# A planned instruction order, planned again with other durations: four graph layers on one core

## The chip, the cores and the metric

The kernel runs on one core of one Trainium2 chip. The core has a matrix engine (TensorE, PE in the profile; its weight loads are listed apart as PEld), a vector engine (VectorE, DVE), a scalar engine (ScalarE, ACT), GpSimd (POOL) and a queue for transfers (SyncE, SP). They run side by side and wait for each other through semaphores. The metric is the time of one execution on the device, in microseconds (us).

## The reference, cut to what matters

128 graphs of 64 nodes with 256 features go through four layers in float32. Each layer ends with a residual and a layer norm.

```python
# layer 0: a gated unit, five rounds with the same gates and another message weight each
A = (adj != 0)
h = x
for l in range(5):
    m = einsum('bnd,de->bne', h, weight[l])
    agg = einsum('bij,bid->bjd', A, m)
    h = gru_cell(agg, h, w_ih, w_hh, b_ih, b_hh)
x = layernorm(x + h * mask)
# layer 1: neighbour sum, then a two-layer network with RMS norm and SiLU, 256 -> 1024 -> 256
agg = epsilon * x + adj @ x
x = layernorm(x + silu(rmsnorm(agg @ W1 + b1)) @ W2 + b2)
# layer 2: log map, neighbour sum, exponential map, projection onto a ball (norms, artanh, tanh)
x = layernorm(x + project(expmap0(adj @ logmap0(x))))
# layer 3: attention with weights mask * exp(e_i + f_j), rows normalized
h = x @ W_w.T + W_b
x = layernorm(x + (u / u.sum(-1)) @ h)        # u = adj * exp(logits)
```

## The kernel before

The graphs form 16 groups of 8. A group is one stream of operations: five gated rounds, the network, the log and exponential maps, the attention, and four layer norms. Groups don't depend on each other except through shared buffers and the eight banks of matmul output. Nothing is issued while the program is described: each operation is put down with its engine, an estimated duration, and what it reads and writes. Some operations (copies out of the banks, scaled copies, the rows of a norm) can be done by ScalarE or VectorE and are put down with both.

```python
def dve(n, run, w, r):
    flow.op("DVE", 0.16 + 0.00105 * n, run, w, r)
def act(n, run, w, r):
    flow.op("ACT", 0.27 + 0.00077 * n, run, w, r)
def copied(n, o, i, w, r):
    flow.either([("ACT", 0.27 + 0.00077 * n, lambda: nc.scalar.copy(o(), i())),
                 ("DVE", 0.16 + 0.00105 * n, lambda: nc.vector.tensor_copy(o(), i()))], w, r)
def scaled(n, o, i, scale, bias, w, r):
    flow.either([("ACT", 0.27 + 0.00077 * n, lambda: nc.scalar.activation(o(), i(), AF.Identity, bias=bias(), scale=scale())),
                 ("DVE", 0.16 + 0.00105 * n, lambda: nc.vector.tensor_scalar(o(), i(), scale(), bias(), OP.mult, OP.add))], w, r)
```

A planner then plays the program forward with these durations. `clock` is when each engine is next free, `at` when an operation's inputs are there. At every step it takes the operation that can start first; ties, and the choice between groups, go by a rank. From the end of one operation to the start of one that needs it on another engine, a passing (`hop`) is added.

```python
            for s in range(self.first, min(self.first + flow.WINDOW, len(self.queues))):
                for e, q in self.queues[s].items():
                    opened = False
                    for _, o in zip(range(flow.AHEAD[e]), q):
                        t = max(clock[e], at[o.id])
                        # ... a free bank, or a free transfer slot, where o needs one
                        key = (t + o.ways[e][0] - min(w[0] for w in o.ways.values()) if len(o.ways) > 1 else t, *rank(s, o))
                        if best is None or key < best[0]:
                            best = key, o, e, t
            # ...
            end = t + o.ways[eng][0]
            clock[eng] = end
            # ...
            for u in o.then:
                need[u.id] -= 1
                at[u.id] = max(at[u.id], end + flow.hop(eng, u.eng))

    HOPS = {"from PE": 0.25, "to PE": 0.3, "else": 0.1}
    WINDOW, STRETCH, WIDTH, LAG = 4, 25.0, 8, 40.0
    ENDGAME = 350.0

    def hop(self, e, to):
        if e == to:
            return 0.0
        return self.HOPS["from PE" if e == "PE" else "to PE" if to == "PE" else "else"]
```

Up to four groups are open at once (`WINDOW`). The search keeps 8 partial plans (24 in the last 350 us of matmul work), lets each go on for a stretch under three different ranks, and keeps those with the lowest bound on the end. The best plan fixes the order of issue on each engine and the engine of each shared operation. The chip then runs that order; real durations and real semaphores decide the times.

```python
        ranks = (lambda s, o: (s, o.n), lambda s, o: (s if o.kb else -s, o.n), lambda s, o: (self.LAG * s - o.way, s, o.n))
        plans, until = [Plan(self)], 0.0
        while any(p.left for p in plans):
            late = until > self.work - self.ENDGAME
            until += self.STRETCH / 2 if late else self.STRETCH
            found = {}
            for p in plans:
                for rank in ranks:
                    c = p.copy()
                    if c.advance(until, rank):
                        found.setdefault((round(c.bound(), 3), c.left), c)
            plans = [found[k] for k in sorted(found)[:self.WIDTH * (3 if late else 1)]]
```

A layer norm is, for four rows of blocks `b`: two small DVE operations per block for mean and variance, one more, a power on POOL, the offset on DVE, and four shared operations for the rows.

```python
            for b in range(NB):
                dve(256, lambda b=b: nc.vector.bn_stats(st[:, b, :], y[:, b, :]), [(st, b)], [(y, b)])
                dve(4, lambda b=b: nc.vector.bn_aggr(mv[:, b, :], st[:, b, :]), [(mv, b)], [(st, b)])
            # ... variance + eps on DVE
            pool(1.1, lambda: nc.gpsimd.tensor_tensor(rstd[:, :m, :], ve[:, :m, :], pow2[:, :m, :], OP.pow), [rstd], [ve])
            # ... offset on DVE
            for b in range(NB):
                scaled(256, lambda b=b: o[:, b, :], lambda b=b: y[:, b, :], lambda b=b: rstd[:, 0, b:b + 1],
                       lambda b=b: off[:, b:b + 1], [(o, b)], [(y, b), off, rstd])
```

Names that return below: `p_u`, `p_v`, `p_w`, `p_r`, `p_in`, `p_hn` are banks of the gated rounds; `hnb`, `hr` are shared copies out of such banks; `U`, `V`, `Z`, `R` hold the gates; `tA`, `tB` and `t` are sums and differences made by DVE as matmul inputs; `ps_hid`, `p_1h`, `p_uh`, `p_vh`, `p_wh`, `hid`, `ps_o`, `xb` belong to the network; `ser`, `fac`, `tan`, `ps_sup` to the maps; `ps_a`, `hw`, `ps_att` to the attention; `x_n` are the rows of a norm.

Of the kernel before, what the change touches and what calls it, by code (L numbers as in the profile page):

```python
# [13 lines left out]
AF = mybir.ActivationFunctionType  # L14
OP = mybir.AluOpType
# [37 lines left out]
class Plan:  # L53
# [25 lines left out]
    def advance(self, until, rank):  # L79


        flow, need, at, clock, banks = self.flow, self.need, self.at, self.clock, self.banks
        while self.left and clock["PE"] < until:
            best = None
# [5 lines that stand above are left out]
                        if o.opens is not None:  # L90
                            if opened or not banks or need[o.id]:
                                opened = True
                                continue
                            t = max(t, banks[0])
                        elif need[o.id]:
                            continue
                        elif o.kb and e != "POOL":
                            t = max(t, self.lands[0])
                        key = (t + o.ways[e][0] - min(w[0] for w in o.ways.values()) if len(o.ways) > 1 else t, *rank(s, o))
                        if best is None or key < best[0]:  # L100
                            best = key, o, e, t
            if best is None:
                return False
            _, o, eng, t = best
            for e in o.ways:
                self.queues[o.stream][e].remove(o)
            self.order.append((eng, o))
            end = t + o.ways[eng][0]
            clock[eng] = end
            if eng == "PE":  # L110
                self.done += o.us
            if o.opens is not None:
                banks.pop(0)
            for b in o.bufs:
                n = self.uses.get(b, b.left) - 1
                self.uses[b] = n
                if not n:
                    banks.append(end + flow.hop(eng, "PE"))
                    banks.sort()
            if o.kb:  # L120
                self.bus = max(self.bus, end + flow.DMA[0]) + o.kb / flow.DMA[1]
                end = self.bus + flow.DMA[2]
                if o.eng != "POOL":
                    self.lands = [*self.lands[1:], end]
# [3 lines that stand above are left out]
            self.left -= 1  # L128
            while self.first < len(self.queues) and not any(self.queues[self.first].values()):
                self.first += 1  # L130
        return True
# [12 lines left out]
class Flow:  # L144
# [10 lines left out]

    AHEAD = {"PE": 32, "DVE": 10, "ACT": 10, "POOL": 4, "SP": 2}

    HOPS = {"from PE": 0.25, "to PE": 0.3, "else": 0.1}


    DMA = (2.0, 330.0, 1.0)
# [51 lines left out]

    def hop(self, e, to):
        if e == to:
            return 0.0
        return self.HOPS["from PE" if e == "PE" else "to PE" if to == "PE" else "else"]

    def ways(self):
# [41 lines left out]
def kernel(  # L261
# [31 lines left out]
    nc = tc.nc  # L293
# [19 lines left out]
    flow = Flow(tc)  # L313
# [6 lines left out]
    def bank(name):  # L320
        return Buf(lambda: psum.tile([P, 512], F32, tag="bank", name=name), bank=True)
# [4 lines left out]
    def unit(tag, s, name, shape=(P, R), bufs=1):  # L326

        t = f"{tag}{s}"
        return Buf(lambda: work.tile(list(shape), F32, tag=t, name=name, bufs=bufs), slot=(t, bufs))


    def matmul(o, lhsT, rhs, k, nk):
        return nc.tensor.matmul(o, lhsT, rhs, start=(k == 0), stop=(k == nk - 1))  # L333

    def pe(n, run, w, r):
        flow.op("PE", {512: 0.86, 256: 0.435, 128: 0.23, 1: 0.21}.get(n, 0.3), run, w, r)
# [2 lines left out]
        flow.op("PE", 0.11, run, w, r)  # L339

    def dve(n, run, w, r):
        flow.op("DVE", 0.16 + 0.00105 * n, run, w, r)

    def act(n, run, w, r):
        flow.op("ACT", 0.27 + 0.00077 * n, run, w, r)

    def copied(n, o, i, w, r):

        flow.either([("ACT", 0.27 + 0.00077 * n, lambda: nc.scalar.copy(o(), i())),  # L349
                     ("DVE", 0.16 + 0.00105 * n, lambda: nc.vector.tensor_copy(o(), i()))], w, r)  # L350

    def scaled(n, o, i, scale, bias, w, r):

        flow.either([("ACT", 0.27 + 0.00077 * n, lambda: nc.scalar.activation(o(), i(), AF.Identity, bias=bias(), scale=scale())),  # L354
                     ("DVE", 0.16 + 0.00105 * n, lambda: nc.vector.tensor_scalar(o(), i(), scale(), bias(), OP.mult, OP.add))], w, r)

    def pool(us, run, w, r=()):
        flow.op("POOL", us, run, w, r)
# [161 lines left out]
    for l in range(L):  # L520
        ps = bank("ps_wmT")
# [9 lines left out]
        for k in range(KD):  # L531
            for i, n in ((0, 2 * D), (1, D)):
                ps = bank("ps_wmih")
# [78 lines left out]
    def group(g):  # L612
        s = g % NF

        def tiny(name, shape=(P, NB), dt=F32):
            t = f"{name}{s}"
            return Buf(lambda: small.tile(list(shape), dt, tag=t, name=f"{name}_{g}"), slot=(t, 2))

        def u(tag, name, shape=(P, R)):
            return unit(tag, s, f"{name}_{g}", shape, bufs(tag))  # L620

        def rows(tag, name):
            return u(tag, name, (P, NB, D))
# [14 lines left out]
        def rows_of(src, n):  # L638

            ps = bank("ps_hr")  # L640
            for j in range(2):
                for c in range(KD):
                    turn(lambda j=j, c=c: nc.tensor.transpose(  # L643
                        ps[:, j * D + c * P:j * D + (c + 1) * P],
                        src[:, c, (2 * n + j) * P:(2 * n + j + 1) * P], ident.tile()), [ps], [(src, n)])
            return ps
# [46 lines left out]
        if g == NG - 2:  # L693


            for k in range(KD):
                w = unit("h", (NG - 3) % NF, f"w1_{k}", (P, H), 2)
# [4 lines left out]
        ps = bank("ps_adjT")  # L702
# [129 lines left out]
        for n in range(2):  # L832
            ps = rows_of(hT, n)
            for j in range(2):
                b = 2 * n + j
# [91 lines left out]
        ps = bank("ps_ss")  # L927
# [10 lines left out]
        for c in range(KH):  # L938
# [4 lines left out]
            th = u("VZR"[c % 3], f"th{c}")  # L943
# [5 lines left out]
        for h in range(NB // 2):  # L949
            ps = bank("ps_o1")  # L950
            for j in range(2):
                b = 2 * h + j
# [4 lines left out]
            for j in range(2):  # L957
                b = 2 * h + j
                dve(256, lambda ps=ps, b=b, j=j: nc.vector.scalar_tensor_tensor(
                    y1[:, b, :], ps[:, j * D:(j + 1) * D], 0.5, xb[:, b, :], OP.mult, OP.add), [(y1, b)], [ps, (xb, b)])  # L960
        xn = tiny("n")
        x2 = layer_norm(y1, "A", "n1", xn)


        rn, fac, n2, ser = (tiny(t) for t in ("rn", "fac", "n2", "ser"))
        near = tiny("near", dt=I32)
# [11 lines left out]
        def series():  # L978
# [5 lines left out]
                  for q in (11, 9, 7, 5, 3)),  # L984
                v.tensor_add(ser.tile(), ser.tile(), one4),
                v.scalar_tensor_tensor(near.tile(), xn.tile(), SERIES_BELOW, one4, OP.is_lt, OP.mult)]
        dve(1250, series, [n2, ser, near], [xn])
        dve(4, lambda: nc.vector.scalar_tensor_tensor(fac.tile(), fac.tile(), 0.5, rn.tile(), OP.mult, OP.mult),
            [fac], [fac, rn])
        dve(4, lambda: nc.vector.copy_predicated(fac.tile(), near.tile(), ser.tile()), [fac], [fac, near, ser])  # L990
        tan = rows("B", "tan")
        for b in range(NB):
            flow.either([
                ("DVE", 0.37, lambda b=b: nc.vector.tensor_scalar(tan[:, b, :], x2[:, b, :], fac[:, b:b + 1], None, OP.mult)),
                ("ACT", 0.47, lambda b=b: nc.scalar.activation(tan[:, b, :], x2[:, b, :], AF.Identity, scale=fac[:, b:b + 1]))],
                [(tan, b)], [(x2, b), fac])
        us = tiny("ss")
        sup = [bank("ps_sup") for _ in range(NB // 2)]
        for h in range(NB // 2):
            for j in range(2):  # L1000
                b = 2 * h + j
                pe(256, lambda b=b, j=j, ps=sup[h]: matmul(
                    ps[:, j * D:(j + 1) * D], adjT[:, b, :], tan[:, b, :], 0, 1), [sup[h]], [adjT, (tan, b)])
            for j in range(2):
                b = 2 * h + j
# [3 lines left out]
        un, unb, th, urn = tiny("n"), tiny("n2"), tiny("th"), tiny("rn")  # L1009
# [12 lines left out]
                v.scalar_tensor_tensor(un.tile(), un.tile(), MAX_NORM, one4, OP.mult, OP.min),  # L1022
                v.tensor_mul(th.tile(), th.tile(), un.tile())]
        dve(4, lambda: nc.vector.reciprocal(urn.tile(), unb.tile()), [urn], [unb])
        dve(800, onto_ball, [th, un], [th, un, urn])
        y2 = rows("y", "y2")
        for b in range(NB):
            dve(256, lambda b=b, ps=sup[b // 2]: nc.vector.scalar_tensor_tensor(
# [11 lines left out]
        for b in range(NB):  # L1040
            ps = bank("ps_a")
            for k in range(KD):
                pe(256, lambda ps=ps, b=b, k=k: matmul(
                    ps[:, :D + 2], x3T[:, k, b * P:(b + 1) * P], wattT[:, k, :], k, KD), [ps], [(x3T, b // 2), wattT])
            act(4, lambda ps=ps, b=b: nc.scalar.activation(
                hw[:, b, D:], ps[:, D:D + 2], AF.Exp, bias=cs.tile()), [(hw, b)], [ps, cs])
            flow.either([
                ("ACT", 0.47, lambda ps=ps, b=b: nc.scalar.activation(
                    hw[:, b, :D], ps[:, :D], AF.Identity, scale=hw[:, b, D:D + 1])),
                ("DVE", 0.43, lambda ps=ps, b=b: nc.vector.tensor_scalar(  # L1050
                    hw[:, b, :D], ps[:, :D], hw[:, b, D:D + 1], None, OP.mult))], [(hw, b)], [ps, (hw, b)])
        dve(1030, lambda: nc.vector.tensor_add(x3.tile(), x3.tile(), over(wb_r.tile(), NB)), [x3], [x3, wb_r])
        y3 = rows("y", "y3")
# [1 line left out]
        for b in range(NB):  # L1055
            ps = bank("ps_att")
# [7 lines left out]
        o = layer_norm(y3, "A", "n3")  # L1064
# [38 lines left out]
```

## Time and profile before

| | |
|---|---|
| time, median of 3 | 2431.84 us (2430.58 to 2432.48) |
| span of the profiled execution | 2430.5 us |
| PE, PEld busy | 99%, 87% |
| DVE, ACT, POOL busy | 78%, 47%, 8% |
| mean granted TensorE clock | 0.994 |
| mean DMA rate | 15 GB/s |

A line of a group reads: line and engine, operation, what it writes and reads, shapes, count, then busy time and mean duration of one in ns, then the idle time of the engine ahead of it and what ended that. Records overlap on an engine, as the next operation may start before the last one has been recorded as ended, so the distance between starts says more than the duration. Two groups that can run on either engine show this division of work before:

```profile
L354 ACT ACTIVATE hnb<-p_hn,half_b 128x256 f32<-128x256 f32 x232 | 101.6, 472 | 81.4 <-PE p_hn L663 67.4 <-DVE hnb L355 13.0 <-DVE Z L776 0.7
...
L354 ACT ACTIVATE x_n<-y,off,rstd 128x256 f32<-128x256 f32 x78 | 42.9, 593 | 44.2 <-DVE off L684 44.1
```

```profile
L355 DVE TENSOR_SCALAR hnb<-p_hn,half_b 128x256 f32<-128x256 f32 x88 | 41.4, 480 | 19.6 <-PE p_hn L663 10.7 <-ACT hnb L354 8.5
L355 DVE TENSOR_SCALAR x_n<-y,rstd,off 128x256 f32<-128x256 f32 x114 | 40.8, 409 | 0.5
```

### The profile page before, as it was taken

The page shows a single profiled execution, that of the slowest core. Times are in us where ns is not written, and L with a number is a line of the kernel's source. Part 1 is how long each engine was busy: PE and PEld are TensorE (multiplying, and loading weights), DVE is VectorE, ACT ScalarE, POOL GpSimd, SP SyncE. Part 2 cuts the span into 40 slices and gives each one's busy share as a digit, 9 for nine tenths or more (in the row PEclk, how much of TensorE's full clock was granted, in tenths as well). Part 3 has the DMA queues.
Part 4 walks back from the last instruction along what each step waited for, and adds up shares of the span by engine and source line. Part 5 has one row for each costly group of instructions (what it writes and reads, how often), then busy time and mean ns, then how long its engine had stood idle before and what let it go on. Part 6 is the DMA issues. An engine that isn't in the chain of part 4 may idle for free.

```text
span 2430.5 us, 32703 instructions
## 1 busy us (share of the span) xinstructions
PE 2394.7 (99%) x12258; PEld 2102.9 (87%) x12258; DVE 1893.4 (78%) x4097; ACT 1147.1 (47%) x2408; POOL 188.2 (8%) x144
## 2 busy tenths in 40 slices
PE   9999999999999999999999999999999999999995
PEld 7888888888888888888888888888888888888864
DVE  3668787887888877778777887888787787878777
ACT  4434544444444444454444545455444544445453
POOL 4000000000100000000000100000000000000011
PEclk9999999999999999999999999999999999999997
DMA  4000000000000000000000000000000000000000
GB/s 127 3 1 12 1 29 1 18 12 1 29 1 27 3 18 11 1 27 3 16 14 1 29 1 27 3 19 11 1 29 1 18 12 1 27 9 18 9 9 18
DMA packets 39725, 36.21 MB, mean 15 GB/s; under 512 B 9956, under 2 KB 38656, under 8 KB 39568
## 3 DMA queue, kind: packets, MB, share of 16 engines
q1 hardware_dynamic: 37840, 32.25, 4.2%
q8 instruction: 97, 1.59, 0.3%
q10 hardware_dynamic: 1328, 1.31, 0.2%
q0 software_dynamic: 400, 0.57, 0.1%
q14 instruction: 60, 0.49, 0.1%
HBM read 25.74 MB, written 8.39 MB: 14 GB/s over the span
## 4 chain that ended last, share of the span: by engine, by line
PE 94%; DVE 4%; ACT 1%; DMA 1%; issue 0%; POOL 0%; SPq 0%; POOLq 0%; ACTq 0%; DVEq 0%
PE p_v L663 11%; PE p_w L663 11%; PE p_in L663 11%; PE p_r L663 11%; PE p_hn L663 11%; PE ps_o L333 9%; PE ps_agg L333 6%; PE p_u L663 6%; PE ps_hr L643 3%; PE ps_a L333 2%; PE p_wh L882 2%; PE p_vh L882 2%; PE p_1h L882 2%; PE ps_T L633 1%; PE ps_att L333 1%; PE p_uh L882 1%
## 5 line engine op out<-in xcount | busy, mean ns | idle before, releaser
L663 PE MATMUL p_hn<-hT,w_hn 128*128 128x256 f32 x1280 | 322.8, 380 | 0.0
L663 PE MATMUL p_in<-agg,w_in 128*128 128x256 f32 x1280 | 315.4, 379 | 0.0
L663 PEld LDWEIGHTS p_in<-agg,w_in 128*128 128x128 f32 x1280 | 240.2, 190 | 31.1
L663 PEld LDWEIGHTS p_hn<-hT,w_hn 128*128 128x128 f32 x1280 | 227.9, 191 | 22.7
L333 PE MATMUL ps_o<-w2s,hid 128*128 128x256 f32 x1024 | 231.2, 379 | 0.0
L333 PEld LDWEIGHTS ps_o<-w2s,hid 128*128 128x128 f32 x1024 | 193.9, 190 | 27.3 <-issue 1.2
L678 POOL TENSOR_TENSOR rstd<-ve,pow 128x4 f32<-128x4 f32 (+1 forms) x64 | 82.5, 1289 | 1491.6 <-DVE ve L676 1484.0
L767 ACT ACTIVATE V<-V,half_b 128x256 f32<-128x256 f32 x160 | 72.7, 500 | 199.2 <-DVE V L763 199.0
L663 PE MATMUL p_u<-tA,s 128*128 128x256 f32 x640 | 158.1, 381 | 1.4 <-DVE tA L746 0.6
L663 PE MATMUL p_w<-tA,s 128*128 128x256 f32 x640 | 158.1, 379 | 0.0
L663 PE MATMUL p_r<-hT,a 128*128 128x256 f32 x640 | 156.9, 379 | 0.0
L663 PE MATMUL p_r<-agg,a 128*128 128x256 f32 x640 | 156.7, 379 | 0.0
L663 PE MATMUL p_v<-tB,s 128*128 128x256 f32 x640 | 155.4, 379 | 0.0
L663 PE MATMUL p_v<-tB,na 128*128 128x256 f32 x640 | 154.5, 379 | 0.0
L663 PE MATMUL p_w<-hT,s 128*128 128x256 f32 x640 | 154.3, 379 | 0.0
L349 ACT COPY agg<-ps_agg 128x512 f32<-128x512 f32 x154 | 89.9, 584 | 114.2 <-PE ps_agg L333 98.8
L333 PEld LDWEIGHTS ps_agg<-edge,hr 128*128 128x128 f32 x1024 | 136.1, 191 | 6.6
L354 ACT ACTIVATE hnb<-p_hn,half_b 128x256 f32<-128x256 f32 x232 | 101.6, 472 | 81.4 <-PE p_hn L663 67.4
L333 PE MATMUL ps_agg<-edge,hr 128*128 128x128 f32 x1024 | 138.8, 275 | 0.0
L663 PEld LDWEIGHTS p_u<-tA,s 128*128 128x128 f32 x640 | 119.3, 190 | 21.0 <-DVE tA L746 2.3
L663 PEld LDWEIGHTS p_v<-tB,s 128*128 128x128 f32 x640 | 120.9, 190 | 16.3 <-PE ps_att L333 0.2
L663 PEld LDWEIGHTS p_w<-hT,s 128*128 128x128 f32 x640 | 120.7, 190 | 16.0
(233 smaller groups left out, 4686.5 us busy)
## 6 DMA issues: line engine op xcount, KB each, us to landing
x<-in_x_dram SPq DMA_DIRECT2D x16, 512.0 KB, 3.6
xr<-in_x_dram SPq DMA_DIRECT2D x16, 512.0 KB, 3.6
out_dram<-x_n SPq DMA_DIRECT2D x16, 512.0 KB, 2.9
edge<-in_adj_dram SPq DMA_DIRECT2D x32, 64.0 KB, 2.3
wm<-in_L_gnn_weight_dram SPq DMA_DIRECT2D x5, 256.0 KB, 5.3
w2s<-in_L_gnn_W_dram SPq DMA_DIRECT2D x1, 1024.0 KB, 10.0
w<-in_L_gnn_W_dram SPq DMA_DIRECT2D x2, 512.0 KB, 3.5
w_in_L_gnn_w_hh_dram<-in_L_gnn_w_hh_dram ACTq DMA_DIRECT2D x1, 512.0 KB, 5.2
```

What stands on the lines that cost most here:

```text
L333: return nc.tensor.matmul(o, lhsT, rhs, start=(k == 0), stop=(k == nk - 1))
L349: flow.either([("ACT", 0.27 + 0.00077 * n, lambda: nc.scalar.copy(o(), i())), ("DVE", 0.16 + 0.00105 * n, lambda: nc.vector.tensor_copy(o( ...
L354: flow.either([("ACT", 0.27 + 0.00077 * n, lambda: nc.scalar.activation(o(), i(), AF.Identity, bias=bias(), scale=scale())), ("DVE", 0.16 ...
L633: turn(lambda j=j, c=c: nc.tensor.transpose(ps[:, c * HR + j * P:c * HR + (j + 1) * P], src[:, 2 * n + j, c * P:(c + 1) * P], ident.tile() ...
L643: turn(lambda j=j, c=c: nc.tensor.transpose(ps[:, j * D + c * P:j * D + (c + 1) * P], src[:, c, (2 * n + j) * P:(2 * n + j + 1) * P], iden ...
L663: pe(256, lambda c=c, k=k: nc.tensor.matmul(ps[:, c * HR:(c + 1) * HR], w[:, k, c * P:(c + 1) * P], v(k), start=first and c == k == 0, sto ...
L678: pool(1.1, lambda: nc.gpsimd.tensor_tensor(rstd[:, :m, :], ve[:, :m, :], pow2[:, :m, :], OP.pow), [rstd], [ve])
L767: act(256, lambda c=c: nc.scalar.activation(o[:, c, :], src(c), AF.Tanh, bias=half_b[:, i * KD + c:i * KD + c + 1], scale=0.5), [(o, c)], ...
L882: pe(256, lambda c=c: nc.tensor.matmul(ps[:, c * HR:(c + 1) * HR], w1f[:, w, (2 * q + c) * P:(2 * q + c + 1) * P], v[0](), start=first and ...
```

## The change

The planner gets other constants. Operations of DVE and ACT get shorter fixed parts, closer to the distance between starts in the trace; an operation that needs the one before it on the same engine is given a passing of 0.12 us (none on PE), and the passings between engines are longer. Of an operation with two engines, the start on DVE is rated 0.4 us later than it is, so that ACT takes it unless it would start more than that behind DVE; before, the difference of the two durations was added to the slower. A few single durations follow. The operations themselves and their dependences stay as they are; the order of issue and the division of shared operations come out of the search anew.

```diff
-                        key = (t + o.ways[e][0] - min(w[0] for w in o.ways.values()) if len(o.ways) > 1 else t, *rank(s, o))
+                        key = (t + flow.SOONER if len(o.ways) > 1 and e == "DVE" else t, *rank(s, o))
...
-    HOPS = {"from PE": 0.25, "to PE": 0.3, "else": 0.1}
+    HOPS = {"from PE": 0.3, "to PE": 0.3, "else": 0.2, "own": 0.12}
+    SOONER = 0.4
...
         if e == to:
-            return 0.0
+            return 0.0 if e == "PE" else self.HOPS["own"]
...
     def dve(n, run, w, r):
-        flow.op("DVE", 0.16 + 0.00105 * n, run, w, r)
+        flow.op("DVE", 0.105 + 0.00105 * n, run, w, r)
     def act(n, run, w, r):
-        flow.op("ACT", 0.27 + 0.00077 * n, run, w, r)
+        flow.op("ACT", 0.15 + 0.00077 * n, run, w, r)
... copied() and scaled() alike: 0.27 -> 0.15 for ACT, 0.16 -> 0.105 for DVE
-        dve(1250, series, [n2, ser, near], [xn])
+        dve(1150, series, [n2, ser, near], [xn])
... the rows of tan: DVE 0.37 -> 0.3, ACT 0.47 -> 0.37
-        dve(800, onto_ball, [th, un], [th, un, urn])
+        dve(900, onto_ball, [th, un], [th, un, urn])
... the rows of hw: ACT 0.47 -> 0.37, DVE 0.43 -> 0.37
```

More of the change, by code (lines that the diff above doesn't have):

```diff
@@ L341, in dve @@
     def dve(n, run, w, r):
-        flow.op("DVE", 0.16 + 0.00105 * n, run, w, r)
+        flow.op("DVE", 0.105 + 0.00105 * n, run, w, r)
     def act(n, run, w, r):
-        flow.op("ACT", 0.27 + 0.00077 * n, run, w, r)
+        flow.op("ACT", 0.15 + 0.00077 * n, run, w, r)
     def copied(n, o, i, w, r):
-        flow.either([("ACT", 0.27 + 0.00077 * n, lambda: nc.scalar.copy(o(), i())),
-                     ("DVE", 0.16 + 0.00105 * n, lambda: nc.vector.tensor_copy(o(), i()))], w, r)
+        flow.either([("ACT", 0.15 + 0.00077 * n, lambda: nc.scalar.copy(o(), i())),
+                     ("DVE", 0.105 + 0.00105 * n, lambda: nc.vector.tensor_copy(o(), i()))], w, r)
     def scaled(n, o, i, scale, bias, w, r):
-        flow.either([("ACT", 0.27 + 0.00077 * n, lambda: nc.scalar.activation(o(), i(), AF.Identity, bias=bias(), scale=scale())),
-                     ("DVE", 0.16 + 0.00105 * n, lambda: nc.vector.tensor_scalar(o(), i(), scale(), bias(), OP.mult, OP.add))], w, r)
+        flow.either([("ACT", 0.15 + 0.00077 * n, lambda: nc.scalar.activation(o(), i(), AF.Identity, bias=bias(), scale=scale())),
+                     ("DVE", 0.105 + 0.00105 * n, lambda: nc.vector.tensor_scalar(o(), i(), scale(), bias(), OP.mult, OP.add))], w, r)
     def pool(us, run, w, r=()):
@@ L993, in group @@
             flow.either([
-                ("DVE", 0.37, lambda b=b: nc.vector.tensor_scalar(tan[:, b, :], x2[:, b, :], fac[:, b:b + 1], None, OP.mult)),
-                ("ACT", 0.47, lambda b=b: nc.scalar.activation(tan[:, b, :], x2[:, b, :], AF.Identity, scale=fac[:, b:b + 1]))],
+                ("DVE", 0.3, lambda b=b: nc.vector.tensor_scalar(tan[:, b, :], x2[:, b, :], fac[:, b:b + 1], None, OP.mult)),
+                ("ACT", 0.37, lambda b=b: nc.scalar.activation(tan[:, b, :], x2[:, b, :], AF.Identity, scale=fac[:, b:b + 1]))],
                 [(tan, b)], [(x2, b), fac])
@@ L1047, in group @@
             flow.either([
-                ("ACT", 0.47, lambda ps=ps, b=b: nc.scalar.activation(
+                ("ACT", 0.37, lambda ps=ps, b=b: nc.scalar.activation(
                     hw[:, b, :D], ps[:, :D], AF.Identity, scale=hw[:, b, D:D + 1])),
-                ("DVE", 0.43, lambda ps=ps, b=b: nc.vector.tensor_scalar(
+                ("DVE", 0.37, lambda ps=ps, b=b: nc.vector.tensor_scalar(
                     hw[:, b, :D], ps[:, :D], hw[:, b, D:D + 1], None, OP.mult))], [(hw, b)], [ps, (hw, b)])
```

## The prediction

> **What bounds the kernel now.** I read the page first, then the busy time by stretches, the waits of TensorE, the groups by form, and the timeline of a steady stretch and of the end. Two lines of the page:
>
> ```profile
> PE 2394.7 (99%) x12258; PEld 2102.9 (87%) x12258; DVE 1893.4 (78%) x4097; ACT 1147.1 (47%) x2408; POOL 188.2 (8%) x144
> ...
> PE 94%; DVE 4%; ACT 1%; DMA 1%; issue 0%; POOL 0%; SPq 0%; POOLq 0%; ACTq 0%; DVEq 0%
> ```
>
> TensorE (PE) is busy in 99% of the span and makes up 94% of the chain that ended last. Busy time alone could hide small waits, because a matmul of 256 columns lasts 379 ns in the groups but is followed by the next one sooner. So I took the cadence from a long piece of the chain:
>
> ```profile
> 845.81 13.81 PE ps_o L333 x64
> ...
> 1235.19 2.23 PE ps_agg L333 x20
> ```
>
> 13.81 / 64 = 216 ns for 256 columns, 2.23 / 20 = 111 ns for 128 columns. The groups by form hold 9016 matmuls of 256 columns, 2624 of 128, 384 of 257 or 258, 104 of 512 and 128 of one column. At 216, 111, 217, 430 (2.58 us for 6 in the chain) and about 100 ns that is 1947 + 291 + 83 + 45 + 13 = 2379 us. The change alters no matmul. So at most 2430.5 - 2379 = 51 us, 2.1% of the span, is not matmul work. The stretches say where it lies:
>
> ```profile
> 0.00:50.00 50.00, 46.60 (x216) 34.06 (x217) 17.42 (x47) 20.36 (x50) 17.27 (x23) 1.00 0.45 135
> ...
> 2300.00:2350.00 50.00, 46.03 (x185) 30.36 (x185) 35.83 (x63) 26.67 (x49) 7.56 (x4) 0.97 0.03 11
> 2350.00:2400.00 50.00, 40.35 (x167) 31.34 (x165) 41.45 (x130) 23.85 (x49) 6.29 (x5) 0.89 0.00 1
> 2400.00:2430.50 30.50, 14.61 (x64) 12.14 (x64) 22.17 (x86) 12.12 (x28) 4.72 (x4) 0.72 0.10 35
> ```
>
> Columns: the stretch, its length, then busy time with the count for PE, PEld, DVE, ACT, POOL, then the granted TensorE clock, DMA share, GB/s. Visible idle of PE is 3.4 us at the start and 3.97 + 9.65 + 15.89 = 29.5 us in the last 130 us. The stretch from 50 to 2300 us is busy for 2247.12 of 2250 us, so it lacks 2.9 us in all. The end is where the schedule loses:
>
> ```profile
> PE ps_T L633 <- ACT x_n L354: 5.3, 1, 5.3
> PE ps_sup L333 <- ACT tan L995: 3.6, 1, 3.6
> PE ps_sup L333 <- DVE tan L994: 3.0, 1, 3.0
> PE ps_hid L333 <- DVE aggm L350: 2.5, 1, 2.5
> ...
> PE ps_hr L643 <- DVE hT L788: 1.4, 1, 1.4
> ```
>
> All five are one-time waits after 2300 us: norms and the series of the last two groups, with no matmuls of other groups left to put between.
>
> **What the Trainium skill says.** The skill's "Perfetto Trace Analysis", section "Identifying the Most-Contended Engine", says that matmul busy share doesn't tell the distance to the limit; hence the count by cadence. It agrees in kind: weight loads are at 87% where matmuls are at 99%, yet the cadence shows the steady part full. The same page, "Optimizing Scalar/DVE Operations", says that the profiled latency of a vector or scalar operation is longer than its hold on the engine because the acknowledged write overlaps with the next one, and that work may go to the scalar engine when the vector engine is saturated. The trace agrees on the first: a 512-column vector operation lasts 690 ns but starts come every 605 ns (below). The second has no purchase here, since DVE at 78% isn't the bound. The skill's "TensorE: Matmul & The Clock Gate", section "What's actually happening", says that idling lowers TensorE's clock. The granted clock of 0.97, 0.89 and 0.72 in the last three stretches agrees; waits at the end cost a little twice.
>
> **The change part by part.** No operation is added or removed. Constants of a planner that fixes the order of issue change, and some 1,250 operations that two engines can run are dealt out by a new rule.
>
> *Durations.* A 512-column DVE operation was planned as 0.16 + 0.00105 x 512 = 0.698 us and becomes 0.643; a 256-column ACT operation falls from 0.467 to 0.347; a 512-column one from 0.664 to 0.544. The timelines show:
>
> ```profile
> 1302.43 0.69 DVE L746 TENSOR_TENSOR tA<-ps_agg,agg 128x512 f32<-128x512 f32 x1
> 1303.16 0.69 DVE L746 TENSOR_TENSOR tA<-hT,tA 128x512 f32<-128x512 f32 x1
> 1303.77 0.69 DVE L782 TENSOR_TENSOR hT<-hT,R 128x512 f32<-128x512 f32 x1
> ...
> 1311.91 0.84 ACT L354 ACTIVATE hnb<-p_hn,half_b 128x256 f32<-128x256 f32 x2 [8.44 <-PE p_hn L663]
> ...
> 2381.88 1.09 ACT L354 ACTIVATE x_n<-xb,off,rstd 128x256 f32<-128x256 f32 x2 [8.26 <-DVE n L967]
> ```
>
> DVE starts are 0.73 us apart where the second needs the first and 0.61 where it doesn't; the new model says 0.643 + 0.12 = 0.76 and 0.64, the old one 0.70 for both. Better. For ACT, two in a row end in 0.84 us at 472 ns each, a hold of 0.37; model 0.347, good. For normalized rows the hold is 1.09 - 0.59 = 0.50, which the old 0.467 met and the new 0.347 doesn't. The nine-operation series runs 2383.34 to 2384.88, 1.54 us, in the old plan 1.47, in the new 1.31. So the model gets better for the common case and worse for a few.
>
> *Longer passings.* 0.2 instead of 0.1 us between ACT, DVE and POOL, 0.3 from PE, 0.12 on one engine. They make up for shorter durations and ask for slack ahead of matmuls. In the steady part this can win part of the 2.9 us of visible idle and of about as much again hidden behind modelled ends (the start-to-start times from 100 to 2300 us exceed the cadence by some 5 us): I take 2 us.
>
> *The lean to ACT.* DVE now runs 88 of 320 hnb, 150 of 256 normalized rows, 46 of 64 tan, 27 of 64 hw, 32 of 128 hr. The old rule preferred DVE by 0.04 us for 256 columns; the new one takes it only if ACT would start over 0.4 us later. I estimate 150 to 200 moved: 0.41 us each off DVE, 60 to 80 us, to about 75%; 0.5 us each onto ACT, 75 to 100 us, to about 51%. Neither was the bound, so in the steady part it is worth nothing directly.
>
> *The end.* It decides. The four rows of a norm are now split two and two, ending after 1.09 us. Under the new rule, with both engines free, ACT takes the first (0), the second (0.35, still below 0.4), DVE the third, and ACT the fourth (0.69 against 0.37 + 0.4): three holds of 0.5 and the 0.09 of latency, 1.6 us. Lost: 0.5 us in each of three norms and tan, 2 us. Against it, DVE is busy for 27.3 of the 33 us between 2384 and 2417, and each row that leaves frees 0.35 us for the other group's chain, 1 to 2 us. About even. What remains is the order itself: between 2300 and 2384 PE loses 1.4 + 2.5 us in waits and about 2 us to the slower clock; a plan that sees the passings should keep 2 to 3 us of that.
>
> Sum: 2 + 2.5 + 0 = 4.5 us less than 2431.84 us: 2427 us.
>
> **The rivals.** (1) The plan is already at its limit: interior waits were 1.4 us over four waits for the matrix sums, so there is nothing to find, and the end is set by 46 us of dependent small operations from the last output matmul (about 2384 us) to the last store. Time: 2431, within 1 us. The 99% speaks for it. (2) The lean slows the end: ACT is where the planner now underestimates (0.347 against 0.50 us), its table loads of 1.28 us also lie there, and the last two groups meet on it. Loss of 3 to 8 us: 2435 to 2440. The 8.26 us of ACT idle ahead of the last norms speaks against it. (3) The search happens on a better ending, with the last two groups further apart, so that one's matmuls fill the other's 5.3, 3.6 and 3.0 us: 10 to 14 us, 2418 to 2422. Such a search over sums of estimates is erratic, which widens the range.
>
> **Range and chances.** To gain 2% the kernel would have to lose 48.6 of its 51 us without matmul work, the last chain included: 0.01. To lose 2% it would have to add as much to waits that are now 36 us: 0.01. Within 2%: 0.98. The range is set by rivals 3 and 2: 2416 to 2437 us; I put gain at about two in three.
>
> **What would show it.** PE's idle between 50 and 2300 us at or below 2 us and matmul counts unchanged: steps one and two right. DVE's busy time near 1820 and ACT's near 1235 us: the lean as sized. Norms in the end with three rows on ACT: the split as worked out. PE's idle after 2300 us within 3 us of 29.5. The prediction is wrong if steady PE idle rises above 8 us (the plan trusts ACT too much), or if that at the end changes by more than 10 us either way.

## The result, and the profile after

The changed kernel takes 2449.7 us (2449.4 to 2450.4 over 4 runs) against 2432.0 for the kernel before on the same chip: ratio 1.0074, 95% interval 1.0057 to 1.0092. It is slower by 17.7 us, where 2427 was predicted with a range of 2416 to 2437. The page of the changed kernel, busy time and the chain by engine:

```profile
PE 2406.7 (98%) x12258; PEld 2103.6 (86%) x12258; DVE 1729.5 (71%) x3812; ACT 1260.6 (52%) x2695; POOL 176.9 (7%) x144
...
PE 90%; ACT 4%; DVE 4%; issue 1%; POOL 0%; DMA 0%; POOLq 0%; SPq 0%; ACTq 0%; DVEq 0%
```

The same 12258 matmuls are now busy for 2406.7 us instead of 2394.7. That already tells of lost time: a matmul of 256 columns is recorded for 379 ns at a cadence of 216, so a wait below some 160 ns doesn't show as idle time but as less overlap. Stretches of the changed kernel, with the columns as before:

```profile
100.00:2300.00 2200.00, 2190.36 (x11287) 1934.18 (x11286) 1581.83 (x3423) 1134.01 (x2428) 132.74 (x98) 1.00 0.04 12
```

```profile
2300.00:2350.00 50.00, 48.70 (x220) 36.63 (x218) 37.55 (x70) 28.80 (x57) 3.38 (x2) 1.00 0.07 22
2350.00:2400.00 50.00, 47.06 (x197) 35.86 (x198) 35.18 (x89) 27.32 (x45) 7.01 (x5) 0.97 0.00 1
2400.00:2447.50 47.50, 23.18 (x85) 17.29 (x83) 26.90 (x128) 26.07 (x62) 7.64 (x7) 0.76 0.07 22
```

After 2300 us, PE is idle for 1.3 + 2.9 + 24.3 = 28.5 us, against 29.5 before: the end is not where the time went. From 100 to 2300 us it gets through 11287 matmuls, where the same stretch of the kernel before holds

```profile
100.00:2300.00 2200.00, 2197.12 (x11373) 1950.59 (x11372) 1749.20 (x3729) 1044.79 (x2192) 143.42 (x99) 1.00 0.04 12
```

86 fewer, at about 0.2 us some 17 us. Below, **steady loss** means this: over all matmuls that start between 100 and 2300 us, the distance to the next start less the cadence (216, 111, 217, 430 ns by columns, 110 for one column). It is 6.1 us before and 22.7 after; the difference of 16.6 is nearly the whole 17. The rest cancels: at the end 3.9 us more above the cadence, and 3.2 less after the last matmul.

The waits of PE in this stretch of the changed kernel (waiting group, what it waited for, sum, times, longest):

```profile
PE p_vh L885 <- DVE t L881: 3.3, 5, 1.0
PE p_wh L885 <- DVE t L881: 3.2, 4, 1.1
PE ps_sup L336 <- ACT tan L998: 1.3, 5, 0.3
```

The kernel before has these there:

```profile
PE p_uh L882 <- DVE t L878: 1.4, 4, 0.6
PE p_u L663 <- DVE tA L746: 0.6, 1, 0.6
PE p_u L663 <- ACT junk_a L1006: 0.5, 1, 0.5
```

By steady loss, p_wh takes 5.0 us, p_vh 4.7, ps_T 3.0 and ps_sup 2.8: matmuls of the network, the norms and the maps, which follow on a norm. Of the 3.1 us at ps_agg, 2.5 are neighbour sums of the gated rounds (0.4 before). The other matmuls of these rounds (p_u, p_v, p_w, p_r, p_in, p_hn, ps_hr) fell from 4.6 to 3.4, so the rounds as a whole lose 5.9 us, against 5.0 before. The division of work, groups of the changed kernel:

```profile
L357 ACT ACTIVATE hnb<-p_hn,half_b 128x256 f32<-128x256 f32 x301 | 127.2, 473 | 80.2 <-PE p_hn L666 79.6
...
L357 ACT ACTIVATE x_n<-y,off,rstd 128x256 f32<-128x256 f32 x165 | 86.1, 592 | 28.3 <-DVE off L687 28.3
```

With those that read xb, 229 of 256 rows of norms run on ACT, where it was 106.

### The profile page after: what moved, and what is told of

It reads as the page before. It is cut to its first block, busy times and chain, and to the rows that moved or that the text cites. A ratio compares the mean times of both kernels' runs of the same rounds, so it can differ in the third digit from the quotient of the medians.

```text
span 2447.5 us, 32804 instructions
## 1 busy us (share of the span) xinstructions
PE 2406.7 (98%) x12258; PEld 2103.6 (86%) x12258; DVE 1729.5 (71%) x3812; ACT 1260.6 (52%) x2695; POOL 176.9 (7%) x144
## 4 chain that ended last, share of the span: by engine, by line
PE 90%; ACT 4%; DVE 4%; issue 1%; POOL 0%; DMA 0%; POOLq 0%; SPq 0%; ACTq 0%; DVEq 0%
PE p_r L666 11%; PE p_in L666 10%; PE p_w L666 10%; PE p_v L666 10%; PE p_hn L666 10%; PE ps_o L336 9%; PE ps_agg L336 6%; PE p_u L666 5%; PE ps_hr L646 3%; PE ps_a L336 2%; PE p_wh L885 2%; PE p_vh L885 2%; PE p_1h L885 2%; ACT x_n L357 1%; PE ps_hid L336 1%; PE ps_sup L336 1%
## 5 line engine op out<-in xcount | busy, mean ns | idle before, releaser
L681 POOL TENSOR_TENSOR rstd<-ve,pow 128x4 f32<-128x4 f32 (+1 forms) x64 | 76.5, 1195 | 1559.1 <-DVE ve L679 1550.6
L357 ACT ACTIVATE hnb<-p_hn,half_b 128x256 f32<-128x256 f32 x301 | 127.2, 473 | 80.2 <-PE p_hn L666 79.6
L779 DVE SCALAR_TENSOR_TENSOR R<-R,hnb 128x512 f32<-128x512 f32 x80 | 56.5, 707 | 114.5 <-ACT R L770 113.9
L770 ACT ACTIVATE R<-p_r,half_b 128x256 f32<-128x256 f32 x160 | 67.8, 470 | 133.9 <-PE p_r L666 133.8
```

Source lines behind the costliest of these rows:

```text
L357: flow.either([("ACT", 0.15 + 0.00077 * n, lambda: nc.scalar.activation(o(), i(), AF.Identity, bias=bias(), scale=scale())), ("DVE", 0.105 ...
L770: act(256, lambda c=c: nc.scalar.activation(o[:, c, :], src(c), AF.Tanh, bias=half_b[:, i * KD + c:i * KD + c + 1], scale=0.5), [(o, c)], ...
L779: dve(512, lambda: nc.vector.scalar_tensor_tensor(t.tile(), t.tile(), 1.0, hnb[:, :, half(n)], OP.add, OP.mult), [t], [t, (hnb, (n, 0)), ( ...
```

## The experiments

Every theory had to say why matmuls come late, those that follow on a norm above all. **A**: rows queue on ACT, which the lean brought about. **B**: the plan believes rows on ACT shorter than they are. **C**: any touched constant throws the search elsewhere (scatter). **D** and **E**, formed later: a plan made with short durations has no reserve, that is, no room for an operation that ends a little later than planned. **F**: a delay no plan knows. Ratios are to the kernel before on the same chip.

**t1 to t4, the change in parts.** t1 is the change with the old rule, t2 the kernel before with

```diff
+ key = (t + flow.SOONER if len(o.ways) > 1 and e == "DVE" else t, *rank(s, o))   # SOONER = 0.4
```

t3 the kernel before with only the new passings, t4 with only the new durations.

> The changed kernel with the old rule for shared operations (new durations and passings stay). Theory A, the lean is the cause, as rows of norms and of tan queue on ACT and reach the next matmuls late: 2428 to 2435 us, TensorE's time above its cadence between 100 and 2300 us back from 22.7 to under 9 us, rows of norms on ACT near 106 of 256. Theory B, the plan trusts ACT durations that are too short (0.347 us against a hold of 0.50 us): still 2443 to 2450 us. Theory C, the search lands at random whatever constant is touched: anything from 2425 to 2450 us, unrelated to the rows on ACT.

> The kernel before with only the new rule for shared operations. Theory A: 2442 to 2452 us, over 200 of 256 rows on ACT, steady TensorE loss of 15 us or more. Theory B: 2430 to 2436 us, since the old ACT durations of 0.467 us are near the hold. Theory C: anything from 2425 to 2450 us.

> The kernel before with only the longer passings between and on engines. Theories A and B: 2426 to 2434 us, the steady loss not above 6 us. Theory C: anything from 2425 to 2450 us.

> The kernel before with only the shorter durations. Theory A: 2428 to 2436 us. Theory B: 2440 to 2450 us, with waits for ACT at the norms. Theory C: anything from 2425 to 2450 us.

| run | us | ratio (95%) | steady loss |
|---|---|---|---|
| t1 | 2443.6 | 1.0051 (1.0036 to 1.0066) | 16.5 |
| t2 | 2448.9 | 1.0074 (1.0059 to 1.0089) | 21.9 |
| t3 | 2440.7 | 1.0039 (1.0025 to 1.0053) | 12.7 |
| t4 | 2529.1 | 1.0403 (1.0387 to 1.0418) | 95.5 |

Each part alone is slower and the parts don't add: 17, 9 and 97 us alone, 18 together. Of the expectations, t1 came out as B has it, t2 as A (with 218 rows on ACT), t3 as C alone allows, and t4 as none: no theory of that time holds for all four. t1 was not the clean test I meant: with the new durations a row costs 0.347 us on ACT and 0.374 on DVE, so the old rule prefers ACT too, with 186 rows there; still, the new rule adds 6 us to it (2443.6 to 2449.7). t4 is the surprise. Its waits of PE between 100 and 2300 us are mostly with DVE in the gated rounds, few of them with rows on ACT:

```profile
PE ps_hr L646 <- DVE hT L791: 9.8, 16, 1.1
PE p_wh L885 <- DVE t L881: 7.4, 8, 2.3
PE p_v L666 <- DVE V L766: 5.2, 9, 1.2
```

So shorter durations without longer passings are harmful by far, and the passings repair most of that harm: t1, which differs from t4 by them alone, is 85 us faster. That fits the trace: between DVE operations of which the second needs the first, starts are 0.73 us apart, and t4 plans 0.643 (the kernel before 0.698).

**t5 and t6, rows on ACT.** t5 plans rows at the distance between starts that the trace has:

```diff
-        flow.either([("ACT", 0.15 + 0.00077 * n, lambda: nc.scalar.activation(o(), i(), AF.Identity, ...
+        flow.either([("ACT", 0.5 if n == 256 else 0.15 + 0.00077 * n, lambda: nc.scalar.activation(o(), ...
-                ("ACT", 0.37, lambda b=b: nc.scalar.activation(tan...
+                ("ACT", 0.42, lambda b=b: nc.scalar.activation(tan...
```

t6 keeps the order found for the changed kernel and only then moves rows:

```diff
+                flow.ops[-1].fixed = ("ACT", "DVE")[b % 2]     # for each row of a norm
...
+                eng = o.fixed or eng                            # when the plan is issued
```

> The changed kernel, planned with the hold of rows on ACT as the trace has it: 0.50 us for a row of a norm, 0.42 for one of tan, in place of 0.347 and 0.37; passings and the lean stay. Theory B (the plan trusts rows on ACT too much, so matmuls behind norms are issued too early): 2428 to 2437 us, steady loss of TensorE (100 to 2300 us, time above its cadence) from 22.7 to under 10 us. Theory D (all short durations without slack are at fault, rows only show it first): 2440 to 2448 us, the loss moves to other waits. Theory C (scatter of the search): 2432 to 2450 us.

> The plan of the changed kernel, its order kept; after the search two rows of each norm are given to DVE and two to ACT. No other search result enters, so scatter is excluded. Theory A (rows queue on ACT): the waits behind norms (transposes, aggregations, matrix sums) go, 8 to 13 us less than the changed kernel, 2437 to 2442 us. If rows on ACT are not the cause: within 3 us of 2449.7, or slower, as DVE gets work at places not planned for.

t5: 2441.0 us, 1.0039 (1.0024 to 1.0054), steady loss 14.1, with 218 rows on ACT: 8.6 of the 16.6 us that the change added go when the plan knows what a row takes, though the rows stay there. That is short of what B asked for, and within what D did. t6: 2451.2 us, 1.0082 (1.0065 to 1.0099), 24.9, with 128 rows on ACT. The loss at ps_T fell from 3.0 to 1.4, that at p_wh rose from 5.0 to 6.7: what ACT is spared, DVE seems to lack. Theory A's gain of 8 to 13 us didn't come; as DVE got rows for which the order had no place, this doesn't show that rows on ACT cost nothing.

**t7 and t8, scatter and truth.** t7 is the kernel before with a search step of 24 us for 25. t8 is a plan with holds and passings as measured, with the old rule:

```diff
+    HOPS = {"from PE": 0.3, "to PE": 0.3, "else": 0.15, "own": 0.12}
+        flow.op("DVE", 0.08 + 0.00105 * n, run, w, r)
+        flow.op("ACT", 0.2 + 0.00084 * n, run, w, r)
+    copies on ACT 0.09 + 0.00077 * n; rows 0.5 on ACT, 0.34 on DVE; hnb 0.38 and 0.4; tan 0.42 on ACT; series 1330, onto_ball 960 columns
```

> The kernel before with the same durations and rules, but a search that prunes every 24 us of matmul work instead of 25: nothing is modelled otherwise, so this measures scatter. Theory C: over 5 us away from 2431.8 us. Theories A, B and D: within 5 us.

> A plan with holds and passings both as the trace has them: DVE 0.08 us + 1.05 ns a column, ACT 0.2 us + 0.84 ns a column from SBUF, 0.50 us for a row of a norm, 0.48 for a copy out of a bank; passings 0.3, 0.15 and 0.12 us; the old rule for shared operations. Theory B: 2424 to 2432 us, steady loss at or below the 6.1 us of before. Theory D: 2435 to 2450 us, as a plan without slack stalls. Theory C: 2425 to 2450 us.

t7: 2429.9 us, 0.9993 (0.9984 to 1.0001). The division of rows came out the same as before (106 on ACT), so the two plans have much in common; it speaks against C, but weakly. t8: 2437.9 us, 1.0028 (1.0018 to 1.0038), steady loss 18.2. The plan truest to the trace is slower than the old one, whose durations were too long.

**t9 to t12, a reserve.** Here theory E took form. One line is added to a planned operation:

```diff
+        ways = [(eng, us if eng in ("PE", "SP") else us * 1.07, run) for eng, us, run in ways]
```

t9 is the change with 1.07, t10 the kernel before with 0.9, t11 is t8 with 1.1, t12 is t5 with 1.1.

> The changed kernel, every planned duration of DVE, ACT and POOL 7% longer; rule, passings and matmuls as in the change. Theory E (a plan is judged by its own idle alone, so once that is zero nothing asks for a reserve; the old durations held a reserve over the real holds that the new ones gave up): steady loss of TensorE from 22.7 to under 14 us, 2434 to 2442 us. Theory A (the lean itself): within 3 us of 2449.7.

> The kernel before, every planned duration of DVE, ACT and POOL 10% shorter, old rule and old passings. Theory E: the reserve is gone, steady loss from 6 to over 20 us, 2445 us or more. Theories A and C: within 6 us of 2431.

> The plan fitted to the trace (t8), every planned duration of DVE, ACT and POOL 10% longer. Theory E: steady loss from 18 to under 7 us, 2424 to 2430 us, so at or below the kernel before. If a plan only gains by being true: 2438 us or more, as t8 was truer.

> The changed kernel with the true hold of rows on ACT (t5) and every planned duration of DVE, ACT and POOL 10% longer; the lean to ACT stays at 0.4 us. Theory E: steady loss from 14 to under 7 us, 2426 to 2434 us, with over 200 of 256 rows still on ACT. Theory A: 2440 us or more.

| run | us | ratio (95%) | steady loss |
|---|---|---|---|
| t9 | 2437.4 | 1.0023 (1.0014 to 1.0031) | 12.3 |
| t10 | 2480.0 | 1.0199 (1.0184 to 1.0214) | 51.1 |
| t11 | 2431.3 | 0.9997 (0.9988 to 1.0005) | 8.2 |
| t12 | 2422.9 | 0.9963 (0.9950 to 0.9976) | 2.8 |

All four moved the way E says; t9 and t10 lie in its ranges, t11 missed its by 1.3 us (and 8.2 is above 7), t12 is 3 us better than its own. Seven percent more gives back 12 of 17.7 us; ten percent less on the kernel before costs 48. t12 beats both kernels and computes all that they do. Its page and its steady stretch:

```profile
PE 2396.5 (99%) x12258; PEld 2103.7 (87%) x12258; DVE 1745.7 (72%) x3852; ACT 1243.3 (51%) x2653; POOL 179.2 (7%) x144
```

```profile
100.00:2300.00 2200.00, 2199.17 (x11392) 1953.87 (x11391) 1609.46 (x3484) 1132.44 (x2417) 134.84 (x98) 1.00 0.04 12
```

11392 matmuls, 105 more than in the changed kernel, with DVE and ACT as busy there as in the changed kernel within 28 us. So the load of the engines isn't it; the order is.

The likely reason lies in how plans are ranked: `bound` is in the main the time of PE plus its work left, so plans in which PE is never idle mostly score alike (ties go to the plan with fewer operations left), and nothing asks how close they came to a wait. The planner leaves a start for every operation, and from them the idle time it foresaw for PE between 100 and 2300 us (a plan, no time of the chip), set against the measured steady loss:

```
            before changed   t2    t3    t4    t8    t9   t10   t11   t12   t13
foreseen us    0.0     0.0  12.8  15.0   0.0   0.0   0.2   0.4   0.0   0.0  30.6
measured us    6.1    22.7  21.9  12.7  95.5  18.2  12.3  51.1   8.2   2.8  31.1
```

Eight of these plans foresee next to no idle time and lose from 2.8 to 95.5 us, so that measure doesn't tell them apart. I read it so: with low durations a plan without idle time is soon found, and the search has no more reason to prefer one with room. With durations above the real ones, finding one means that there is room. Where none was found (t2, t3, t13), the idle time is planned in. The room itself was not measured.

**t13 to t15, which engine, and the lean.** t13 is t12 with the old rule; t14 and t15 are the change with 1.1 on DVE or on ACT alone.

> Run t12 with the old rule for shared operations, all else kept. If the lean is what makes room on DVE for a reserve of 10%: 2440 us or more, with TensorE idle that the plan itself foresees. If the lean is indifferent (as the prediction had it): within 4 us of 2422.9. If the lean costs: under 2420 us.

> The changed kernel with planned durations 10% longer on DVE alone. If the reserve that was given up is DVE's (hold 0.605 us, planned 0.698 before and 0.643 after): steady loss from 22.7 to under 13 us, 2434 to 2440 us. If ACT's: within 3 us of 2449.7.

> The changed kernel with planned durations 10% longer on ACT alone. If the reserve that was given up is ACT's (hold 0.41 us for a tanh, planned 0.467 before and 0.347 after): 2438 to 2443 us. If DVE's: within 3 us of 2449.7.

t13: 2460.4 us, 1.0116 (1.0101 to 1.0131), 113 rows on ACT. The lean isn't indifferent: without it the same reserve doesn't fit on DVE. PE waits for DVE:

```profile
PE ps_ss L337 <- DVE ve L680: 7.2, 1, 7.2
PE ps_hr L647 <- DVE hT L792: 2.8, 3, 1.2
```

t14: 2442.7 us, 1.0046 (1.0029 to 1.0062), steady loss 16.3 (I had expected under 13 and at most 2440 us). t15: 2441.9 us, 1.0040 (1.0025 to 1.0055), 16.8. Each gives back 7 to 8 us: the reserve was missing on both engines.

**t16 to t18, a delay that no plan knows.** One wait of p_wh, followed back in the timeline of the changed kernel, ends at this (DVE, POOL and PE rows, each from a timeline of its engine):

```profile
1222.31 2.55 DVE L785 TENSOR_TENSOR hT<-hT,R 128x512 f32<-128x512 f32 x1 [0.23 <-ACT R L783]
1224.79 0.47 DVE L358 TENSOR_SCALAR hnb<-p_hn,half_b 128x256 f32<-128x256 f32 x1
1225.18 0.74 DVE L881 TENSOR_TENSOR t<-aggm 128x256 f32<-128x256 f32 x2
```

```profile
1221.95 2.36 POOL L856 TENSOR_TENSOR xb<-x_n,b_r 128x1024 f32<-128x1024 f32 x1 [3.91 <-ACT x_n L357]
```

```profile
1225.73 0.45 PE L885 MATMUL p_wh<-t,w1f 128*128 128x256 f32 x1 [0.89 <-DVE t L881]
```

An addition that lasts 0.69 us elsewhere takes 2.55, until GpSimd is done. The same edit in three kernels, made after the search, takes GpSimd's addition away; it leaves out the bias b2:

```diff
+        flow.ops[-1].fixed = "SP", lambda: nc.sync.dma_start(xb.tile(), x1.tile())
```

> The changed kernel with its order kept; after the search the addition xb (rows plus a bias, 2.36 us on GpSimd, once a group) is issued as a transfer of the rows, which leaves the bias out. While that addition runs, a DVE operation with both inputs in SBUF lasts 2.55 us instead of 0.69 (16 us over 12 operations in the changed kernel), and the matrix sums behind it come about 1.1 us late. Theory F (the plan knows nothing of this hold-up, and a reserve is what absorbs it): steady loss of TensorE from 22.7 to 12 to 15 us, 2438 to 2443 us, the waits of p_vh and p_wh gone. If the hold-up only coincides: within 3 us of 2449.7.

> The kernel before with the same edit. It has the same hold-up (20.5 us over 13 operations) but a reserve. Theory F: 2428 to 2432 us, hardly a gain. If the hold-up costs TensorE wherever it falls: 2420 us or less.

> Run t12 (reserve of 10%, 13.9 us of hold-up over 13 operations) with the same edit. Theory F: the reserve has absorbed nearly all of it, so 2420 to 2424 us against 2422.9.

t16: 2439.9 us, 1.0034 (1.0021 to 1.0047), steady loss 12.4; p_vh and p_wh no longer lose. t17: 2422.9 us, 0.9964 (0.9950 to 0.9978), 1.0. t18: 2420.2 us, 0.9951 (0.9936 to 0.9966), 0.4. The waits of PE between 100 and 2300 us that t16 keeps:

```profile
PE ps_sup L338 <- ACT tan L1001: 1.3, 5, 0.3
PE ps_agg L338 <- ACT hr L354: 0.6, 3, 0.2
PE p_u L668 <- DVE tA L751: 0.2, 1, 0.2
```

My expectation for t17 was wrong: the kernel before gains 9 us as well (5 in the steady part, 4 at the end), so its reserve did not cover the hold-up. Changed and before without the hold-up lie 2439.9 - 2422.9 = 17.0 us apart, as they did with it. So F explains where the longest waits fall, and 9 to 10 us in either kernel, but not the difference of the times. In the steady part it does explain a share: there the hold-up cost the changed kernel 10.3 us and the kernel before 5.1, so 5 of the 16.6 us; the kernel before also gains 4 us at the end, where the changed one gains nothing, and that evens it out. Of t12 only 2.7 us go, and there the reserve did cover most of it.

## Why the prediction was wrong, point by point

- **The limit by cadence** held: the matmuls are unchanged in number, and no run took less than 2419 us, against 2379 us of pure matmul work. The change also stayed within 2%.
- **Durations and passings** is the step that failed. It reads "the model gets better for the common case and worse for a few", lets the passings "make up for shorter durations", and takes 2 us of gain in the steady part. The steady part lost 16.6. What I treated as an error of the old plan, 0.698 us planned for a hold of 0.605 and 0.467 for one of 0.41, was its reserve; the passings give much of it back (85 us from t4 to t1), but only between dependent operations. t8 to t11 show it from both sides.
- **The lean** was undersized: 150 to 200 operations to be moved, and DVE at 1820 and ACT at 1235 us were forecast. DVE runs 285 fewer instructions and stands at 1729.5, ACT at 1260.6. That it is worth nothing by itself in the steady part doesn't hold either: it costs 6 us with the change's own durations (t1 against the change, steady loss 16.5 to 22.7), 17 us in t2, where the plan foresees 12.8 us of idle time, and carries t12 (37 us against t13).
- **The end** came out even, as sized for rows and DVE. Four rows, not three, run on ACT there, in 2.07 us. The 2.5 us of better order didn't come. With the cost of a norm mis-sized (2.07 us, not 1.6), the even sum is partly luck.
- **Rival 2** had the right suspect, ACT planned at 0.347 for 0.50 us, but at the end and as a queue; t5 shows its share (8.7 us) in the steady part and as a belief of the plan, and t6 gives no sign of the queue. None of the rivals asked what happens when a plan has no room left.
- The prediction named its own failure: steady idle above 8 us. From 100 to 2300 us it is 2200 - 2190.36 = 9.6.

On ACT the new durations aren't closer to the trace in general. The prediction read a hold of 0.37 us from copies out of a bank and called 0.347 good. Activations of 256 columns out of SBUF hold ACT longer; two of them, of 0.50 us each, end after 0.91 in the kernel before:

```profile
1318.37 0.91 ACT L767 ACTIVATE V<-V,half_b 128x256 f32<-128x256 f32 x2 [1.69 <-DVE V L763]
```

That is a hold of 0.91 - 0.50 = 0.41. The new 0.347 lies as far below it as the old 0.467 lay above, and further from the 0.50 of a row than the old one.

Left open: t6 couldn't separate the queue on ACT from the load it put on DVE; scatter of the search was measured with one step only (t7, steady loss 6.1 as before). Against scatter speaks that all eight runs that differ from their own base in durations alone (t4, t5, t9 to t12, t14, t15) moved the steady loss the way E says, by 6 to 89 us.

## What to carry to other kernels

A static order is only as good as the delay it can take. Plan with durations some per cent above the measured ones (7 to 10% more gave back 6 to 11 us of steady loss in t9, t11, t12, t14 and t15) on every engine that feeds the bound one, stop where the plan begins to foresee idle time, and make room by moving work off the fullest helper engine; fitting durations exactly, or judging a plan by its own idle time alone, gave the room away here. Busy time of a pipelined engine that rises with unchanged work is itself a sign of waits.

## What the runs showed of the hardware that was not expected

- GpSimd's addition (2.36 us) held up DVE operations with two inputs in SBUF, by 1.2 to 1.9 us in 8 of 12 cases in the changed kernel; those that read one input from a matmul bank were not held up (in the kernel before, R out of p_in, begun 0.2 to 0.6 us into an addition, lasted its usual 0.69 us four times). In all, 20.5 us over 13 operations before, 16.0 over 12 after. The Trainium skill's "SBUF — State Buffer", section "SBUF: two separate sides", says just this: a GpSimd operation that reads SBUF and a DVE operation with two SBUF inputs exclude each other for a whole instruction, and the first to start has its way. The trace agrees, in both directions: in the kernel before, where such DVE operations got in first, the addition itself took up to 3.28 us. Removing one addition per group was worth 9 us of 2432 in the kernel before, as much as the best order found (t12).
- Hold (start to next start on the engine) and latency (start to the start of what needs it elsewhere) differ by engine and source: a 512-column copy from a bank on ACT holds it for 0.48 us and lets DVE start after 0.62; a 256-column copy out of a bank holds ACT for 0.37, an activation out of SBUF for 0.41, a row of a norm, with two scalar operands, for 0.50.
